# Gated linear attention beside a mixture of experts: the decays between tokens from broadcast loads and a bias, in place of a TensorE product

## The chip, the cores and the metric

One NeuronCore of a Trainium2 chip runs the whole kernel in one launch. The metric is device time in microseconds. The kernel before has a median of 1294.73 us over 9 runs (1287.51 to 1297.57). The engines are named as in the profile: PE is TensorE's matmul (PEld its weight load), DVE is VectorE, ACT is ScalarE, POOL is GpSimd, SP is SyncE, which here only issues DMAs.

## What is computed

The input x is (4, 2048, 256), so 8192 tokens of 256. It is layer-normed, and the output is x plus gated linear attention plus a mixture of experts, both of the normed x.

```python
# attention: 8 heads, keys of 128, values of 64, per sequence of 2048 tokens
q = (x @ Wq).reshape(B, S, H, DK)
k = (x @ Wk).reshape(B, S, H, DK) * DK ** (-0.5)
v = (x @ Wv).reshape(B, S, H, DV)
alpha = jax.nn.sigmoid((x @ Wg + bg) / GATE_NORM)      # one decay per token and head
def step(state, inp):
    qt, kt, vt, at = inp
    state = at[..., None, None] * state + kt[..., None] * vt[:, :, None, :]
    return state, jnp.einsum('bhk,bhkv->bhv', qt, state)
...
return out * sigmoid(x @ Wog) @ Wo
# experts: 64 experts, the 8 best of the 4 best groups per token, 256 places each
buf = zeros(E, CAP + 1, h).at[e, pos_c].set(x[token])[:, :CAP]
y = einsum('eci,eih->ech', silu(g) * u, w_down)
out = zeros(n, h).at[token].add(y_slots * w_slot[:, None])
```

With l(i) the sum of the log decays up to token i of a chunk of 128 tokens, the recurrence inside a chunk is a product of queries and keys, weighted by exp(l(i) - l(j)) for a query i and a key j that is not later than i, and by 0 for a later key. That weight, for four heads at a time, is the tile `dc` (128 keys on the partitions, 4 heads x 128 queries along them), and the change is about how `dc` is made.

## The kernel before, in words

The tokens go in 16 batches of 512 (`front`, `decays`, `back`: layer norm, routing, log decays) and, for the attention, in 32 blocks of 256 tokens, which are two chunks of 128 (`NCK`). A block has two halves of four heads. One *unit* is (block, half, chunk), 128 units in all. For each unit,

- `unit_l` (L889) makes `dc`,
- `unit_a` (L908) makes `sp`, keys times queries, in PSUM,
- `unit_m` (L921) multiplies `dc` by `sp` on VectorE (L924),
- `outputs` (L928) multiplies by the values (L940, result `od`) and adds the carried state times the decayed queries `qt` (L946); it takes two units at a time,
- `states` (L958) carries the state on.

**How `dc` is made before.** `decays` (L418) runs once for each of six groups of batches (1, 1, 2, 4, 4 and 4). The log decays z are split on a coarse grid into two parts (L433, L434). TensorE sums both parts over the tokens of a chunk (`cs`, L437 to L441); ScalarE takes the exponential of the running sum (`le`, for `el`) and of the sum from a token to the chunk's end (`w_end`). VectorE splits each running sum into three bf16 parts (`lt`, L453 to L457). TensorE transposes `le` and `lt`, VectorE copies them out of PSUM (`els` L462, `lts` L471), and SP stores them to DRAM (`el_d`, `lt_d`, L463 and L472). For each block, `load_block` (L778) brings the bf16 parts back with four small DMAs: into `aj` (key side, chunk by chunk) and into 6 rows of `mv` (query side; its other rows hold a fixed -1 per head). `unit_l` is then one bf16 matmul of 512 columns (L894) whose 54 rows add up l(i) - l(j) for four heads in PSUM (`lp`), a Relu with scale -1 (L898), which turns positive differences (later keys) into 0, and an Exp with scale -1 (L899). The mask for later keys is an `affine_select` on POOL (L904) as long as routing runs, and a multiplication by a triangle of ones on VectorE (L902) after that.

**Loads that stay.** `load_el` (L793) loads exp(l(i)) of four heads and two chunks as a broadcast to all 128 partitions: 512 KB a DMA, two DMAs a block. `queries` reads it (L855), and `wall` (L861) copies its last column for `states`, on POOL for the first 16 blocks and on VectorE from then on (`B["aux"]`).

**Order.** `block(s)` (L1026) writes out an order: attention of block s interleaved with projections of block s + 1, and between them `step()`, which advances the side work (layer norm, routing, decays) while there is any, and the experts after that. Block s + 1 is loaded at the head of block s (`load_block`, `load_el` of half 0) and in its middle (`load_el` of half 1). From this, the framework's scheduler makes one fixed list of instructions per engine, by priority and by a simulated time line, and each engine works its list strictly in order. So an instruction may stand well ahead of its place in the program, and one that has to wait holds up all that is behind it on its engine. SP's list holds nearly all loads and stores; POOL's queue issues the experts' gathers (L619) and their accumulating scatters (L697).

**Two long stages.** Up to some 605 us the attention runs beside layer norm and routing; then routing is done, and it runs beside the experts (`if "at" in moe`). PSUM's banks for the projections and `lp` (pool `pj`) are four in the first stage and three in the second. `dc` has a pool of its own with two buffers.

Of the kernel before, what the change touches and what calls it, by code (L numbers as in the profile page):

```python
# [19 lines left out]
P = 128  # L20
# [10 lines left out]
RT = 4  # L31
# [11 lines left out]
CGRID = 1.5 * 2.0 ** 14  # L43
# [5 lines left out]
NPART = 3  # L49
NJ = NPART * H  # L50
KL = 2 * NJ + 2 * NPART

# [19 lines left out]
def gla_moe_kernel(ctx: ExitStack, tc: tile.TileContext, x, Wq, Wk, Wv, Wo, Wg, bg, Wog,  # L72
# [17 lines left out]
    lt_d = [dram.tile([2 * NPART, H, RT, P], BF16, name=f"lt_d{b}") for b in range(NB)]  # L90
# [4 lines left out]
    identb = const.tile([P, P], BF16, name="identb")  # L95
    nc.vector.tensor_copy(identb, ident)
# [15 lines left out]
    w_end = const.tile([P, NB, H, RT], F32, name="w_end")  # L112
# [9 lines left out]


    mz = tmpc.tile([P, H], BF16, name="mz")
    nc.vector.memset(mz, 0.0)
    for q0 in (0, NJ + 2 * NPART):
        for m in range(NPART):
            nc.gpsimd.affine_select(out=mz, in_=mz, pattern=[[-1, H]],
                                    compare_op=ALU.not_equal, fill=-1.0, base=-(q0 + 8 * m),
                                    channel_multiplier=1)  # L130
    NM = 4

    mv_t = [const.tile([P, H, P], BF16, name=f"mv{i}") for i in range(NM)]
    aj_t = [const.tile([P, NCK, P], BF16, name=f"aj{i}") for i in range(2)]
    nc.gpsimd.tensor_copy(mv_t[0], bc(mz, 2, P))
    for t in aj_t:
        nc.vector.memset(t, 1.0)
# [111 lines left out]
    dcp = ctx.enter_context(tc.tile_pool(name="dcp", bufs=2))  # L249
# [33 lines left out]

    lad = r1.tile([P, RT, P], BF16, name="lad")
# [26 lines left out]
    zs = r1.tile([P, NB, H, RT], F32, name="zs")  # L311
    sg = r1.tile([P, NB, H, RT], F32, name="sg")
# [20 lines left out]
    def front(b):  # L333
# [75 lines left out]
        nc.vector.scalar_tensor_tensor(zs[:, b].rearrange("p h t -> p t h"), in0=lg[:, :, E:E + H],  # L409
# [8 lines left out]
    def decays(gi):  # L418

        b0, nb_ = DGROUPS[gi]  # L420
        n = nb_ * H * RT

        z = zs[:, b0:b0 + nb_].rearrange("p b h t -> p (b h t)")
        sm = sg[:, b0:b0 + nb_].rearrange("p b h t -> p (b h t)")
        nc.vector.tensor_scalar(sm, sm, SMIN, None, ALU.max)
        made["ln"] = nc.scalar.activation(sm, sm, AF.Ln).ins
        nc.vector.tensor_scalar(z, z, -UMIN, 0.0, ALU.add, ALU.min)
        nc.vector.tensor_scalar(z, z, LMIN - UMIN, None, ALU.max)
        yield True
        nc.vector.tensor_tensor(z, z, sm, ALU.add)  # L430

        g = dk.tile([P, 2, n], F32, tag="g", name="g")
        nc.vector.tensor_scalar(g[:, 0, :], z, CGRID, CGRID, ALU.add, ALU.subtract)  # L433
        made["g"] = nc.vector.tensor_tensor(g[:, 1, :], z, g[:, 0, :], ALU.subtract).ins  # L434
        yield True
        cs = ps["mo"].tile([P, 4, n], F32, tag="mo", name="cs")
        nc.tensor.matmul(cs[:, 0:2, :].rearrange("p a n -> p (a n)"), lhsT=u_le,  # L437
                         rhs=g.rearrange("p a n -> p (a n)"), start=True, stop=True)
        for q in range(2):
            nc.tensor.matmul(cs[:, 3, :], lhsT=u_le, rhs=g[:, q, :], start=(q == 0), stop=(q == 1))  # L440
        made["cs"] = nc.tensor.matmul(cs[:, 2, :], lhsT=u_gt, rhs=z, start=True, stop=True).ins  # L441

        le = dk.tile([P, n], F32, tag="le", name="le")
        made["le"] = nc.scalar.activation(le.rearrange("p (b t h) -> p b h t", b=nb_, t=RT),
                                          cs[:, 3, :].rearrange("p (b h t) -> p b h t", b=nb_, t=RT), AF.Exp).ins
        made["exp"] = nc.scalar.activation(w_end[:, b0:b0 + nb_].rearrange("p b h t -> p (b h t)"),
                                           cs[:, 2, :], AF.Exp).ins
        lt = dk.tile([P, 2, nb_, NPART, H * RT], BF16, tag="lt", name="lt")
        rs = dk.tile([P, 2, n], F32, tag="g", name="rs")
        by_batch = dict(b=nb_)  # L450
        c4 = cs[:, 0:2, :].rearrange("p a (b n) -> p a b n", **by_batch)
        r4 = rs.rearrange("p a (b n) -> p a b n", **by_batch)
        nc.vector.tensor_copy(lt[:, :, :, 0, :], c4)  # L453
        nc.vector.tensor_tensor(r4, c4, lt[:, :, :, 0, :], ALU.subtract)
        nc.vector.tensor_copy(lt[:, :, :, 1, :], r4)
        nc.vector.tensor_tensor(r4, r4, lt[:, :, :, 1, :], ALU.subtract)
        made["lt2"] = nc.vector.tensor_copy(lt[:, :, :, 2, :], r4).ins  # L457
        yield True
        ep = ps["mo"].tile([n, P], F32, tag="mo", name="ep")
        nc.tensor.transpose(ep, le, ident)  # L460
        els = dk.tile([n, P], F32, tag="ls", name="els")
        nc.vector.tensor_copy(els, ep)  # L462
        nc.sync.dma_start(out=el_d[gi], in_=els)  # L463
        NR = NPART * H * RT
        for i in range(nb_):
            b = b0 + i
            lp = ps["mo"].tile([NR, 2, P], BF16, tag="mo", name="ltp")
            for q in range(2):
                made["ltp"] = nc.tensor.transpose(lp[:, q, :], lt[:, q, i].rearrange("p a n -> p (a n)"), identb).ins
            lts = r2.tile([NR, 2, P], BF16, name="lts")  # L470
            made["lts"] = nc.vector.tensor_copy(lts, lp).ins  # L471
            made["lt"] = nc.sync.dma_start(out=lt_d[b].rearrange("(q a) h c i -> (a h c) q i", q=2), in_=lts).ins  # L472
            yield True
# [292 lines left out]
    def begin_block(s):  # L766
        blk[s] = dict(el=[None, None], wall=[None, None], q=[None, None], k=[None, None], kt=[None, None],
                      v=[None] * NCK, vw=[None] * NCK, oT=[None] * NCK)
        blk[s]["aux"] = nc.gpsimd if s < NB else nc.vector
        b, c0 = s // 2, (s % 2) * NCK  # L770
        if s == 0:
            xs = batch[0]["xT"][:, 0:NCK]
        else:
            xs = xsp.tile([P, NCK, 2, 2, P], F16, name="xs")
            nc.sync.dma_start(out=xs, in_=xT_d[b][:, c0:c0 + NCK])
        blk[s]["x"] = xs[:, :, 0], xs[:, :, 1]

    def load_block(s):  # L778
        if s:
            begin_block(s)  # L780
        b, c0 = s // 2, (s % 2) * NCK
        aj = aj_t[s % 2]
        lt = lt_d[b].rearrange("a h c i -> (a h) c i")
        nc.sync.dma_start(out=aj[0:NJ], in_=lt[0:NJ, c0:c0 + NCK, :])
        nc.sync.dma_start(out=aj[NJ + 2 * NPART:KL], in_=lt[NJ:2 * NJ, c0:c0 + NCK, :])
        mv = []
        for ck in range(NCK):
            t = mv_t[(s * NCK + ck) % NM]
            loaded = nc.sync.dma_start(out=t[NJ:NJ + 2 * NPART], in_=lt_d[b][:, :, c0 + ck, :])
            mv.append(t)  # L790
        blk[s].update(loaded=loaded, aj=aj, mv=mv)
# [32 lines left out]
    def values(s, ck):  # L824
# [11 lines left out]
        if (s * NCK + ck + 1) % (SEQ // P):  # L836
            vwh = vp_.tile([P, H, DV], F16, name="vwh")
            vwl = vp_.tile([P, H, DV], F16, name="vwl")
            vw = w1.tile([P, H, DV], F32, name="vw")
            B["aux"].tensor_tensor(vw, v, bc(w_end[:, b, :, c0 + ck], 2, DV), ALU.mult)  # L840
            nc.scalar.copy(vwh, vw)
            B["aux"].tensor_tensor(vwl, vw, vwh, ALU.subtract)
            B["vw"][ck] = (vwh, vwl)

# [44 lines left out]
    def unit_l(s, half, ck):  # L889

        B = blk[s]
        h0 = half * 4
        lp = ps["pj"].tile([P, 4, P], F32, tag="pj", name="lp")
        nc.tensor.matmul(lp.rearrange("p h i -> p (h i)"), lhsT=B["aj"][:, ck, :],  # L894
                         rhs=B["mv"][ck][:, h0:h0 + 4, :].rearrange("p h i -> p (h i)"),
                         start=True, stop=True)
        dc = dcp.tile([P, 4, P], F32, name="dc")
        nc.scalar.activation(dc, lp, AF.Relu, scale=-1.0)  # L898
        nc.scalar.activation(dc, dc, AF.Exp, scale=-1.0)  # L899

        if "at" in moe:
            nc.vector.tensor_tensor(dc, dc, bc(u_le, 1, 4), ALU.mult)  # L902
        else:
            nc.gpsimd.affine_select(out=dc, in_=dc, pattern=[[0, 4], [1, P]], compare_op=ALU.is_ge,  # L904
                                    fill=0.0, base=0, channel_multiplier=-1)
# [120 lines left out]
    def block(s):  # L1026
# [8 lines left out]
        if n:  # L1035
            load_block(s + 1)
            load_el(s + 1, 0)
        unit_l(s, 0, 1)
# [39 lines left out]
        load_el(s + 1, 1)  # L1078
        unit_l(s, 1, 1)
# [34 lines left out]
    for t in mv_t[1:]:  # L1114
        nc.sync.dma_start(out=t, in_=mv_t[0])
# [54 lines left out]
    with after(made["el"]):  # L1170
        load_block(0)
    with after(blk[0]["loaded"].ins):
        load_el(0, 1)
        nc.sync.dma_start(out=gbias, in_=gate_bias.partition_broadcast(P))
# [86 lines left out]
```

## Time and profile before

| | before |
|---|---|
| median of 9 runs | 1294.73 us |
| the profiled execution | 1291.28 us |
| its span, first to last instruction | 1289.6 us |
| mean granted TensorE clock | 0.996 |
| DMA traffic | 165.36 MB, mean 128 GB/s |
| share of 16 DMA engines: SP's queue, POOL's queue | 28.1%, 20.9% |
| small loads of the decay parts: aj<-lt_d, mv<-lt_d | 64 and 64, 12 KB each |
| broadcast loads: el<-el_d | 64, 512 KB each |

A profile is one execution. Its page gives the busy time of each engine, the chain of work that ended last, and the groups of instructions by source line. A group line reads: line, engine, operation, tile written and tiles read, shapes, count, then busy time, mean duration of one in ns, and the idle time of the engine just before them with what ended it. Matmuls are pipelined: what one costs is seen in the distance of starts, not in its duration. The other engines' back-to-back instructions overlap a little as well. Views of the trace beside the page are the timeline (instructions in order of time), the waits (who waited for whom), and windows (busy time of each engine in a stretch).

### The profile page before, as it was taken

The numbers are of one execution on the slowest core, as the hardware profiler recorded it, in microseconds if no ns is written. First come the engines' busy times: TensorE is split into PE (matmuls) and PEld (weight loads), VectorE is DVE, ScalarE is ACT, GpSimd is POOL, SyncE is SP. The second block draws the span as 40 slices with busy tenths as digits, with TensorE's granted clock in tenths as the row PEclk, the third lists the DMA queues.
The fourth block names the chain that finished last, engine by engine and source line by source line (L and its number), as shares of the span: only waits on it lengthen the run. The fifth ranks groups of instructions, "written<-read, shape, count | busy, mean of one in ns | idle before, by whom it ended". The sixth has DMA issues, their size and how long they took to land.

```text
span 1289.6 us, 34810 instructions
## 1 busy us (share of the span) xinstructions
PE 1205.1 (93%) x13782; PEld 1043.4 (81%) x13783; DVE 997.6 (77%) x2733; ACT 832.4 (65%) x1522; POOL 711.0 (55%) x885
## 2 busy tenths in 40 slices
PE   6789999988999999999899999999999999999997
PEld 6577877777877778788788888888888898888986
DVE  6976877776777777777878788788788897877864
ACT  4576666675666566655667666677677676666764
POOL 1476666664765666643427565636756556555330
PEclk9899999999999999999999999999999999999999
DMA  7534443343233443322646666567767677656531
GB/s 236 157 118 119 128 123 116 114 126 113 72 106 107 126 123 107 107 66 70 171 109 145 147 157 142 139 149 177 142 152 158 148 173 169 136 118 157 103 67 34
DMA packets 148580, 165.36 MB, mean 128 GB/s; under 512 B 32384, under 2 KB 119296, under 8 KB 147712
## 3 DMA queue, kind: packets, MB, share of 16 engines
q1 hardware_dynamic: 114896, 113.57, 28.1%
q0 software_dynamic: 29712, 45.89, 20.9%
q10 hardware_dynamic: 3808, 3.67, 0.8%
q8 instruction: 108, 1.77, 0.6%
q14 instruction: 56, 0.46, 0.1%
HBM read 115.98 MB, written 58.38 MB: 135 GB/s over the span
## 4 chain that ended last, share of the span: by engine, by line
PE 54%; DVE 17%; POOL 13%; ACT 6%; DMA 4%; issue 4%; SPq 1%; another core or an unknown queue 0%; ACTq 0%; POOLq 0%; DVEq 0%
PE pj L269 8%; PE pj L271 8%; PE pj L270 8%; PE od L940 3%; DMA el<-el_d 3%; PE od L946 3%; PE kp L879 2%; PE gu L271 2%; PE gu L269 2%; PE gu L270 2%; POOL ol L985 2%; POOL state L976 2%; PE xet L639 2%; DVE k L221 2%; DVE dc L924 2%
## 5 line engine op out<-in xcount | busy, mean ns | idle before, releaser
L697 POOL DMA_INDIRECT out_dram<-y,idx x128 | 209.8, 1639 | 98.1 <-DMA out_dram<-y,idx 27.5
L619 POOL DMA_INDIRECT xe<-xw_d,idx x128 | 138.2, 1080 | 149.7 <-ACT y L683 112.6
L269 PE MATMUL pj<-xs,wq_h 128*128 128x256 f16 x496 | 136.3, 275 | 5.6 <-ACT dc L898 4.2
L269 PE MATMUL pj<-xs,wk_h 128*128 128x256 f16 x496 | 135.2, 273 | 1.4 <-ACT dc L898 0.8
L270 PE MATMUL pj<-xs,wq_h 128*128 128x256 f16 x496 | 136.0, 274 | 0.0
L271 PE MATMUL pj<-xs,wq_l 128*128 128x256 f16 x496 | 135.9, 274 | 0.0
L270 PE MATMUL pj<-xs,wk_h 128*128 128x256 f16 x496 | 135.2, 273 | 0.8 <-issue 0.7
L271 PE MATMUL pj<-xs,wk_l 128*128 128x256 f16 x496 | 135.2, 273 | 0.1
L221 DVE SCALAR_TENSOR_TENSOR k<-pj,k 128x512 f16<-128x512 f32 x128 | 87.6, 684 | 46.9 <-ACT k L220 46.9
L924 DVE TENSOR_TENSOR dc<-sp,dc 128x512 f32<-128x512 f32 x128 | 87.7, 685 | 32.4 <-PE sp L271 14.6
L940 PE MATMUL od<-dc,v 128*64 128x128 f32 x1024 | 101.5, 280 | 10.4 <-DVE dc L924 9.6
L270 PE MATMUL sp<-ql,k 128*128 128x128 f16 x512 | 96.6, 220 | 15.5 <-DVE ql L221 15.3
L898 ACT ACTIVATE dc<-lp 128x512 f32<-128x512 f32 x128 | 76.1, 595 | 47.3 <-PE lp L894 21.6
L220 ACT ACTIVATE qh<-pj 128x512 f16<-128x512 f32 x128 | 74.7, 592 | 43.6 <-PE pj L271 33.4
L269 PE MATMUL sp<-qh,k 128*128 128x128 f16 x512 | 99.8, 220 | 3.1 <-issue 2.2
L220 ACT ACTIVATE k<-pj 128x512 f16<-128x512 f32 x128 | 75.2, 590 | 42.1 <-PE pj L271 37.4
L271 PE MATMUL sp<-qh,k 128*128 128x128 f16 x512 | 96.5, 220 | 0.7 <-issue 0.7
L946 PE MATMUL od<-qt,state 128*64 128x128 f32 x960 | 93.9, 273 | 0.0
L879 PE MATMUL kp<-identh,k 128*128 128x128 f16 x1024 | 84.5, 221 | 9.3 <-DVE k L221 6.6
L221 DVE SCALAR_TENSOR_TENSOR ql<-pj,qh 128x512 f16<-128x512 f32 x128 | 86.6, 677 | 3.4 <-ACT qh L220 3.3
L855 DVE SCALAR_TENSOR_TENSOR qt<-pj,el 128x512 f32<-128x512 f32 x128 | 86.6, 677 | 0.0
L834 ACT ACTIVATE v<-pj 128x512 f32<-128x512 f32 x64 | 38.2, 598 | 74.4 <-PE pj L271 66.6
(409 smaller groups left out, 4524.0 us busy)
## 6 DMA issues: line engine op xcount, KB each, us to landing
el<-el_d SPq DMA_DIRECT2D x64, 512.0 KB
xw_d<-x SPq DMA_DIRECT2D x16, 512.0 KB
xT_d<-xT SPq DMA_DIRECT2D x16, 512.0 KB
out_dram<-in_L_attn_x_dram SPq DMA_DIRECT2D x16, 512.0 KB
w<-in_L_ffn_w_gate_dram SPq DMA_DIRECT2D x64, 128.0 KB
w<-in_L_ffn_w_up_dram SPq DMA_DIRECT2D x64, 128.0 KB
w<-in_L_ffn_w_down_dram SPq DMA_DIRECT2D x64, 128.0 KB
xs<-xT_d SPq DMA_DIRECT2D x31, 256.0 KB
```

The lines of the kernel that those rows point to most:

```text
L220: return (nc.scalar.activation(hi, t, AF.Copy, scale=scale).ins, nc.vector.scalar_tensor_tensor(lo, in0=t, scalar=scale, in1=hi, op0=ALU.m ...
L221: nc.vector.scalar_tensor_tensor(lo, in0=t, scalar=scale, in1=hi, op0=ALU.mult, op1=ALU.subtract).ins)
L269: nc.tensor.matmul(out_, lhsT=a[0], rhs=b[0], start=first, stop=False)
L270: nc.tensor.matmul(out_, lhsT=a[0], rhs=b[1], start=False, stop=False)
L271: return nc.tensor.matmul(out_, lhsT=a[1], rhs=b[0], start=False, stop=last).ins
L619: in_turn(lambda: nc.gpsimd.indirect_dma_start(out=xe[:, f, :], out_offset=None, in_=xw_d[:, :], in_offset=bass.IndirectOffsetOnAxis(ap=id ...
L697: two = [in_turn(lambda: nc.gpsimd.indirect_dma_start(out=of, out_offset=bass.IndirectOffsetOnAxis(ap=idx[:, e, f:f + 1], axis=0), in_=m[" ...
L855: read = nc.vector.scalar_tensor_tensor(qt, in0=pj, scalar=QFIT, in1=two_heads(el, i), op0=ALU.mult, op1=ALU.mult)
L879: nc.tensor.transpose(kp[:, i, :], k[:, i, :], identh)
L924: anchor.append(nc.vector.tensor_tensor(dc, B["sp"], dc, ALU.mult).ins)
L940: mm = nc.tensor.matmul(od[i * DV:(i + 1) * DV, n, j, :], lhsT=v[:, h0 + 2 * j + i, :], rhs=dc[:, 2 * j + i, :], start=True, stop=first)
L946: mm = nc.tensor.matmul(od[i * DV:(i + 1) * DV, n, j, :], lhsT=state[half][:, 2 * j + i, :], rhs=qt[:, ck, 2 * j + i, :], start=False, sto ...
```

## The change

The log decays are no longer split. `decays` computes, from z itself, the running sums `cs[1]` (for `el`), the sums to the chunk's end `cs[0]` (for `w_end`), and a third sum with the matrix `uq`: the key's own term, relative to the start of the quarter of the chunk (32 tokens) in which the key lies. The third is kept in SBUF for all tokens (`nl`). One more fp32 product per group, with the matrix `tq` of 4 x 128 columns, gives for each quarter g the log decay sums from the start of quarter g to every query i. These go to DRAM (`la_d`) and are loaded for each block and half as `la`: the partitions of quarter g get the rows of quarter g, broadcast to 32 partitions, four DMAs and 512 KB in all. `dc` is then a part of `la` itself: the mask is set first (POOL's `affine_select` fills with -30000, VectorE takes the minimum with a matrix of +30000 and -30000), and ScalarE's Exp adds `nl` as a per-partition bias, one instruction for each head, as the bias differs by head. The clamp of positive differences is gone. The arrays z, sg and `w_end` change the order of their last two dimensions. `load_block`, `aj`, `mv` and their set-up and the pool of `dc` go; `la` has a pool of three buffers.

```diff
-    dcp = ctx.enter_context(tc.tile_pool(name="dcp", bufs=2))
+    lap = ctx.enter_context(tc.tile_pool(name="lap", bufs=3))
...
+    later_ = const.tile([P, P], F32, name="later")
+    nc.vector.tensor_scalar(later_, u_le, -2.0 * NONE, NONE, ALU.mult, ALU.add)
...
+    tq = r1.tile([P, GQ, P], F32, name="tq")
+    for g in range(GQ):
+        nc.vector.tensor_scalar(tq[:, g], u_le, u_le[:, g * Q:g * Q + 1], None, ALU.subtract)
+    uq = r1.tile([P, P], F32, name="uq")
+    nc.vector.tensor_tensor(uq.rearrange("p (g i) -> p g i", g=GQ), bc(u_le[:, 0:P:Q], 2, Q),
+                            u_le.rearrange("p (g i) -> p g i", g=GQ), ALU.subtract)
...
         nc.vector.tensor_tensor(z, z, sm, ALU.add)
-        g = dk.tile([P, 2, n], F32, tag="g", name="g")
-        nc.vector.tensor_scalar(g[:, 0, :], z, CGRID, CGRID, ALU.add, ALU.subtract)
-        made["g"] = nc.vector.tensor_tensor(g[:, 1, :], z, g[:, 0, :], ALU.subtract).ins
         yield True
-        cs = ps["mo"].tile([P, 4, n], F32, tag="mo", name="cs")
...
+        cs = ps["mo"].tile([P, 3, n], F32, tag="mo", name="cs")
+        for k, u in enumerate((u_gt, u_le, uq)):
+            made["cs"] = nc.tensor.matmul(cs[:, k, :], lhsT=u, rhs=z, start=True, stop=True).ins
...
-        nc.vector.tensor_copy(lt[:, :, :, 0, :], c4)
-        nc.vector.tensor_tensor(r4, c4, lt[:, :, :, 0, :], ALU.subtract)
-        nc.vector.tensor_copy(lt[:, :, :, 1, :], r4)
-        nc.vector.tensor_tensor(r4, r4, lt[:, :, :, 1, :], ALU.subtract)
-        made["lt2"] = nc.vector.tensor_copy(lt[:, :, :, 2, :], r4).ins
+        made["lt2"] = nc.vector.tensor_copy(nl[:, b0:b0 + nb_].rearrange("p b t h -> p (b t h)"), cs[:, 2]).ins
...
-        for i in range(nb_):
...
-            for q in range(2):
-                made["ltp"] = nc.tensor.transpose(lp[:, q, :], lt[:, q, i].rearrange("p a n -> p (a n)"), identb).ins
-            lts = r2.tile([NR, 2, P], BF16, name="lts")
-            made["lts"] = nc.vector.tensor_copy(lts, lp).ins
-            made["lt"] = nc.sync.dma_start(out=lt_d[b].rearrange("(q a) h c i -> (a h c) q i", q=2), in_=lts).ins
-            yield True
+        lp = ps["mo"].tile([n, GQ, P], F32, tag="mo", name="lap")
+        made["ltp"] = nc.tensor.matmul(lp.rearrange("n g i -> n (g i)"), lhsT=z,
+                                       rhs=tq.rearrange("p g i -> p (g i)"), start=True, stop=True).ins
+        las = dk.tile([n, GQ, P], F32, tag="las", name="las")
+        made["lts"] = nc.vector.tensor_copy(las, lp).ins
+        made["lt"] = nc.sync.dma_start(out=la_d[gi].rearrange("g n i -> n g i"), in_=las).ins
+        yield True
...
-    def load_block(s):
...
+    def load_la(s, half):
         b, c0 = s // 2, (s % 2) * NCK
...
+        la = lap.tile([P, NCK, 4, P], F32, name="la")
+        gi = max(i for i, g in enumerate(DGROUPS) if g[0] <= b)
+        r0 = ((b - DGROUPS[gi][0]) * RT + c0) * H
+        src = la_d[gi][:, r0:r0 + NCK * H, :].rearrange("g (c h) i -> g c (h i)", h=H)[:, :, half * 4 * P:(half + 1) * 4 * P]
+        for g in range(GQ):
+            blk[s]["loaded"] = nc.sync.dma_start(out=la[g * Q:(g + 1) * Q].rearrange("p c h t -> p c (h t)"),
+                                                 in_=src[g].partition_broadcast(Q))
+        blk[s]["la"][half] = la
...
     def unit_l(s, half, ck):
         B = blk[s]
-        h0 = half * 4
-        lp = ps["pj"].tile([P, 4, P], F32, tag="pj", name="lp")
-        nc.tensor.matmul(lp.rearrange("p h i -> p (h i)"), lhsT=B["aj"][:, ck, :],
-                         rhs=B["mv"][ck][:, h0:h0 + 4, :].rearrange("p h i -> p (h i)"),
-                         start=True, stop=True)
-        dc = dcp.tile([P, 4, P], F32, name="dc")
-        nc.scalar.activation(dc, lp, AF.Relu, scale=-1.0)
-        nc.scalar.activation(dc, dc, AF.Exp, scale=-1.0)
+        b, c = s // 2, (s % 2) * NCK + ck
+        dc = B["la"][half][:, ck]
         if "at" in moe:
-            nc.vector.tensor_tensor(dc, dc, bc(u_le, 1, 4), ALU.mult)
+            nc.vector.tensor_tensor(dc, dc, bc(later_, 1, 4), ALU.min)
         else:
             nc.gpsimd.affine_select(out=dc, in_=dc, pattern=[[0, 4], [1, P]], compare_op=ALU.is_ge,
-                                    fill=0.0, base=0, channel_multiplier=-1)
+                                    fill=NONE, base=0, channel_multiplier=-1)
+        for i in range(4):
+            hh = half * 4 + i
+            nc.scalar.activation(dc[:, i], dc[:, i], AF.Exp, bias=nl[:, b, c, hh:hh + 1])
         B["dc", half, ck] = dc
...
     def block(s):
...
         if n:
-            load_block(s + 1)
+            begin_block(s + 1)
             load_el(s + 1, 0)
+            load_la(s + 1, 0)
...
         load_el(s + 1, 1)
+        load_la(s + 1, 1)
...
-    for t in mv_t[1:]:
-        nc.sync.dma_start(out=t, in_=mv_t[0])
...
     with after(made["el"]):
-        load_block(0)
+        load_la(0, 0)
     with after(blk[0]["loaded"].ins):
         load_el(0, 1)
+        load_la(0, 1)
```

## The prediction

> **What bounds the kernel now.** I read the busy times first, then the chain of work that ended last, then the same chain by stage, and only then the groups of instructions that the change touches. In the first fence the columns after each engine are its busy time and its instructions.
>
> ```profile
> PE 1205.1 (93%) x13782; PEld 1043.4 (81%) x13783; DVE 997.6 (77%) x2733; ACT 832.4 (65%) x1522; POOL 711.0 (55%) x885
> ...
> PE 54%; DVE 17%; POOL 13%; ACT 6%; DMA 4%; issue 4%; SPq 1%; another core or an unknown queue 0%; ACTq 0%; POOLq 0%; DVEq 0%
> ...
> 60.00:605.00 545.00, 507.94 (x6109) 428.92 (x6107) 408.41 (x1238) 347.81 (x613) 337.65 (x582) 1.00 0.38 109
> 605.00:1290.00 685.00, 655.21 (x7310) 578.43 (x7309) 542.70 (x1343) 453.10 (x856) 355.65 (x263) 1.00 0.60 138
> ```
>
> The last two lines are the windows view of the two long stages (length, then busy time of PE, PEld, DVE, ACT and POOL, the granted clock, the DMA share, GB/s): attention with routing, then attention with the experts. PE looks 93 to 96% busy in both, but they have different limits. When I add up the pieces of the chain by stage, PE makes 565.5 of the 685 us (83%) of the late stage, DVE 52.6 (8%) and ACT 24.2. In the middle stage PE makes only 112.7 of 545 (21%), POOL 163.6 (30%), DVE 156.1 (29%), ACT 43.8 (8%) and DMA 31.4, of which 28.1 is the load of el. So TensorE work is worth its time late, and a fifth of it in the middle.
>
> The decay step of a unit (one chunk, four heads) is these lines:
>
> ```profile
> L894 PE MATMUL lp<-mv,aj 128*128 128x512 bf16 x127 | 48.7, 383 | 0.0
> L898 ACT ACTIVATE dc<-lp 128x512 f32<-128x512 f32 x128 | 76.1, 595 | 47.3 <-PE lp L894 21.6 <-PE yp L271 9.4 <-PE pj L271 5.5
> L899 ACT ACTIVATE dc<-dc 128x512 f32<-128x512 f32 x128 | 80.8, 631 | 2.3
> L902 DVE TENSOR_TENSOR dc<-dc,u_le 128x512 f32<-128x512 f32 x63 | 43.2, 685 | 4.2 <-ACT dc L899 3.6 <-issue 0.3
> L904 POOL TENSOR_SCALAR_AFFINE_SELECT dc<-dc 128x512 f32<-128x512 f32 x65 | 42.5, 660 | 35.4 <-ACT dc L899 35.4
> L924 DVE TENSOR_TENSOR dc<-sp,dc 128x512 f32<-128x512 f32 x128 | 87.7, 685 | 32.4 <-PE sp L271 14.6 <-POOL dc L904 14.2 <-PE gu L271 2.4
> ```
>
> The relay PE, ACT, ACT, POOL or DVE, DVE, PE is visible in the idle columns: each engine waits for the one before it.
>
> **What TensorE gives up.** 383 ns is not the price of the product, as matmuls overlap. The timeline has starts:
>
> ```profile
> 901.64 0.38 PE L894 MATMUL lp<-mv,aj 128*128 128x512 bf16 x1
> 901.86 0.27 PE L269 MATMUL pj<-xs,wk_h 128*128 128x256 f16 x1
> ```
>
> The next one starts 0.22 us later; the median over all is 0.216. 128 x 0.217 = 27.8 us, some 13.5 in the middle (62 units) and 13.7 late (63). By the chain's shares that is 13.7 x 0.83 = -11.3 and 13.5 x 0.21 = -2.8. Ends: 0 and -27.8.
>
> **Waits that go.** With no lp, no PSUM bank is held until ScalarE reads it, and the exponential no longer stands behind TensorE. Matmuls that waited for it: od on the product of L924 (PE idle 9.6 us), pj on L898 (5.0). Ends 0 and -14.6; I take a quarter, -4, since such idle time mostly comes back at the next wait.
>
> **The preparation (decays).** Removed on VectorE are the grid split and the three-part split and 16 copies: L433, L434, L453 to L457, L471, in all 19.4 us. Added are 6 copies of 512 columns out of PSUM (nearest: 0.67 us for 64x512 in L542) and 6 small ones (0.22, as L453): 5.3. Net 14 us in the middle, x 0.29 = -4 (ends 0, -14). On TensorE 32 transposes (4.1 us) go and 6 products of 512 fp32 columns come (two 256-column fp32 rows of 282 ns each, 3.4 us): nothing, and they would be 3 us if uncovered.
>
> **ScalarE.** Before: Relu and Exp of 512 columns, which start 0.478 and 0.536 us apart in a row: 1.01 us. After: four Exp of 128 columns with a per-partition bias. No row has that shape. From below: L683 (256 columns, one per-partition operand, from PSUM) steps 0.356 us; from above: L382 (256 columns, two such operands, from SBUF) steps 0.492. 128 columns less are 0.11 us (512 columns more cost 0.44 between L886 and L884), so 0.25 to 0.38 each, 1.0 to 1.53 for four. I take 0.30, between them, as there is one operand but an SBUF source: 1.2, so +0.19 x 128 = +24 us of work (ends 0, +66). ScalarE is 65% busy and has 8% and 3.5% of the chain, so +1.3; all +24 if its idle time were gone.
>
> The Trainium skill (ScalarE: Activation LUTs, "What ACT_TABLE_LOAD costs") speaks against this change: a per-partition operand adds about 93 ns to each instruction, and a small one is mostly fixed cost. By its figures four take 1.18 us and the old pair 1.04, which would be +18 us of work, an estimate; the rows above bracket it, so the sum would stay.
>
> **The loads.** Removed are two 12 KB loads into aj and two into mv per block; added are 64 times 512 KB into la, in four DMAs of 32 partitions. The nearest row is el: also 512 KB, 256 packets of 2,048 bytes, and packets of that size took 102 ns on average in the trace, so 256 x 102 / 16 = 1.64 us of all 16 DMA engines, 105 us over the run. The DMA share rises from 0.38 to about 0.46 and from 0.60 to 0.68: room in both. el's last packet ends 3.2 to 4.5 us behind its issue. On SP, eight issues of 0.37 a block (3.0 us) replace 2.2. They wait for the buffer's last reader, od, and behind them queue the experts' weights; those that were issued at 909 to 911 were used by ScalarE at 918.5, so 7 us cover that. I take +1; ends 0 and +12.6, the chain's whole DMA time late, again.
>
> **The wait that comes.** The mask now comes first, on POOL in the middle and on VectorE late, and depends on nothing but la's landing. What such an instruction does is seen at el: the copy wall on POOL is ordered as early as its load was thought to be there, and POOL stands still.
>
> ```profile
> 100.35 0.36 SPq L799 DMA_DIRECT2D el<-el_d  x1
> ...
> 105.31 0.19 POOL L861 COPY wall<-el 128x8 f32<-128x8 f32 x1 [1.23 <-DMA el<-el_d]
> 105.47 1.16 POOL L842 TENSOR_TENSOR vwl<-vw,vwh 128x512 f16<-128x512 f32 x1
> ...
> POOL wall L861: 33.1, 21
> ```
>
> 33.1 us over 32 loads of el in that stage is 1.03 us a load. Queued behind it are vwl, state and ol, which feed TensorE. If la's first reader waits as long: 32 x 1.03 = 33 us on POOL, x 0.30 = +10; late, 33 us on VectorE, x 0.08 = +2.5. Ends: 0 (la has three buffers and is needed half a block later, so the mask may well be placed late) and +66 (each wait whole on the path). VectorE's instruction itself, min for mult, keeps its 685 ns; POOL's select its 660.
>
> **Start-up.** The first product of L924 starts at 49.5, after POOL's wait for el until 48.6. The split chain goes, 1 MB more of broadcasts comes early. I take -2; ends -5 (the first lp ran at 43.9, and POOL was free to follow at once) and +6.6 (four more loads of 1.64).
>
> **Sum**: -11.3 - 2.8 - 4 - 4 + 1.3 + 1 + 10 + 2.5 - 2 = -9.3. The profiled execution took 1291.3 us (span 1289.6 and 1.7 around it), so 1282.0. It lies 3.4 below the median of the nine runs, 1294.7; for a median I add them: **1285**.
>
> **Rivals.** *All of TensorE's time comes out*: la always lands before anyone looks. For it: the late stage is 83% PE, el there has no wait on VectorE. Against it: VectorE is 79% busy late. 1294.7 - 27.8 - 4 - 2 = 1261. *No change*: VectorE and POOL set the pace as soon as TensorE lets go. For it: 21% in the middle. Then -11.3 is halved and the waits take the rest: 1292 to 1297. *Slower by in-order waits*: la's first reader stops POOL and VectorE at each load, as wall does, and lands later than el, behind it in the queue. The gains are 24.1, the other costs 2.3, so it decides from 21.8 / 64 = 0.34 us a load on the path. With half of the 66 us on the path, 1294.7 - 21.8 + 33 = 1306; with all, 1339. For it: el alone makes 28 us of the middle chain. Against it: POOL's 35.4 us of waiting for L899 go at the same places. *The exponentials do not get cheaper for anyone*: at 1.53 us a unit with its share doubled, +7, 1292; inside "no change".
>
> **Chances.** Forecast 0.40 (1274 to 1290), all of it 0.12, no change 0.10, slower 0.38. Faster by more than 0.3% (about what a measurement of this kernel can tell from no change; 3.9 us) 0.52, within 0.10, slower 0.38. The range goes from just under the full gain, 1258, into the slower case to where some three quarters of la's waits are on the path, 1322.
>
> **What would show it.** Right: no lp; PE busy near 1156 (1205 - 49); a group of 512 exponentials with a mean near 0.4 us; POOL's wait for L899 gone; the late stage shorter by 8 us or more. The wait: idle time before the select (POOL) and the min (VectorE) that a DMA of la ended, 33 us each by my figure. Wrong: if that idle time is over 60 us, or if the weights' wh waits for w by more than its 3.5 us, SP's queue being the cause.

## The result, and the profile after

| | before | after |
|---|---|---|
| median | 1294.17 us (62 runs) | 1364.07 us (19 runs) |
| lowest to highest | 1287.33 to 1302.33 | 1352.78 to 1373.18 |
| span of the profiled execution | 1289.6 us | 1368.0 us |
| mean granted TensorE clock | 0.996 | 0.976 |

The change makes the kernel slower by 5.2%: the ratio is 1.0523, 95% interval [1.0506, 1.0539]. One of the 19 runs after, the highest, was in a slower state, and the ratio is that of the means of the fast runs (that of the two medians is 1.054). The forecast was 1285 with a range up to 1322, so the sign was wrong and the time lies outside the range.

The page of the kernel after, busy times:

```profile
PE 1216.7 (89%) x13623; PEld 1043.3 (76%) x13623; DVE 1003.8 (73%) x2689; ACT 838.4 (61%) x1778; POOL 708.9 (52%) x878
```

TensorE has 159 matmuls less, and yet its busy time is 11.6 us longer; I had expected 49 us less. No engine has become the bound: every busy share fell. What grew is idle time, and with it the time in which TensorE runs at a lower clock.

The windows view of the two long stages, with the columns as in the prediction:

```profile
60.00:605.00 545.00, 489.09 (x5851) 411.89 (x5849) 403.61 (x1160) 338.31 (x712) 329.00 (x573) 0.98 0.48 137
605.00:1290.00 685.00, 618.04 (x6679) 537.76 (x6677) 514.85 (x1307) 427.05 (x918) 345.01 (x261) 0.98 0.65 155
```

In the same 685 us TensorE gets 6679 matmuls done where it did 7310 before. The DMA shares, 0.48 and 0.65, are about what I had forecast (0.46 and 0.68). Starts of the product `dc` times `sp` (L924 before, L891 after) show where time is lost: the first of the 128 starts 2.7 us earlier than before (46.7 against 49.5), the 65th 18.8 later (628.0 against 609.1), the last 74.9 later (1355.3 against 1280.4). So the loss grows over the whole run, and three quarters of it lies in the late stage.

The groups of the decay step, each with the idle time of its engine just before it and what ended it:

```profile
L872 ACT ACTIVATE la<-la,nl 128x128 f32<-128x128 f32 x512 | 160.3, 390 | 108.7 <-POOL la L868 52.4 <-DVE la L866 48.3 <-issue 5.7
L891 DVE TENSOR_TENSOR la<-sp,la 128x512 f32<-128x512 f32 x128 | 87.5, 684 | 37.7 <-PE sp L257 31.3 <-PE kp L849 3.2 <-ACT la L872 2.6
L866 DVE TENSOR_TENSOR la<-la,later 128x512 f32<-128x512 f32 x63 | 41.1, 688 | 51.1 <-DMA la<-la_d 48.6 <-issue 2.4
L868 POOL TENSOR_SCALAR_AFFINE_SELECT la<-la 128x512 f32<-128x512 f32 x65 | 40.8, 649 | 25.2 <-DMA la<-la_d 24.4 <-PE pj L257 0.4 <-issue 0.3
L849 PE MATMUL kp<-identh,k 128*128 128x128 f16 x1024 | 89.5, 222 | 46.0 <-DVE k L207 43.3 <-ACT k L206 0.8 <-ACT res L964 0.5
```

The instructions cost what they should: min 688 ns, select 649, an exponential 390. The waits are the news. VectorE stands still for 48.6 us until a load of la lands, POOL for 24.4; ScalarE, whose exponential is next in its own list, stands still behind them for 52.4 + 48.3 = 100.7 us; and TensorE waits 43.3 us for `k`, which VectorE copies out of PSUM once it is free again. In the kernel before, ScalarE's step waited for TensorE (36.5 us in the three reasons shown), VectorE's mask 3.6 us for ScalarE, and TensorE's `kp` 6.6 us for `k`:

```profile
L879 PE MATMUL kp<-identh,k 128*128 128x128 f16 x1024 | 84.5, 221 | 9.3 <-DVE k L221 6.6 <-ACT dc L898 2.0 <-ACT res L997 0.4
```

The worst of these stops (the second in this fence), in the chain of work that ended last (start, length, what). SP issues the four DMAs of one la, and from then on the chain runs through their landing:

```profile
1064.31 0.45 SPq L759
1064.80 4.50 DMA la<-la_d
1069.42 0.70 DVE la L866
...
1088.33 0.38 SPq L759
1088.75 0.64 SPq L759
1089.43 1.70 SPq L759
1091.18 10.55 DMA la<-la_d
...
1102.46 0.95 DVE wl L683
1103.41 0.60 DVE la L866
```

Above it stands the load before, where the landing takes 4.50 us of the chain; here it takes 10.55. The same moment in the timeline, first VectorE, then TensorE:

```profile
1093.76 0.15 DVE L580 TENSOR_TENSOR idx<-row,place 128x2 int32<-128x2 f32 x1
1101.85 0.69 DVE L866 TENSOR_TENSOR la<-la,later 128x512 f32<-128x512 f32 x1 [7.94 <-DMA la<-la_d]
...
1097.35 0.27 PE L257 MATMUL pj<-xs,wq_l 128*128 128x256 f16 x1
1106.53 1.01 PE L849 MATMUL kp<-identh,k 128*128 128x128 f16 x8 [8.91 <-DVE k L207]
...
1108.19 0.41 PE L256 MATMUL gu<-xel,wh 128*128 128x256 f32 x1
1108.40 0.41 PE L257 MATMUL gu<-xeh,wl 128*128 128x256 f32 x1
```

VectorE idles 7.94 us for a mask whose weights are multiplied only at 1138.9, 37 us later. Behind the mask stands the copy that makes `k`; TensorE's next instruction reads it, and TensorE idles 8.91 us. When it goes on, the matmuls of `gu` start 0.21 us apart; at 1059.8 they started 0.12 apart. The clock records show half clock from 1100.8 on for 10.2 us.

### The profile page after: what moved, and what is told of

It reads as the page before. It is cut to its first block, busy times and chain, and to the rows that moved or that the text cites. A ratio compares the mean times of both kernels' runs of the same rounds, so it can differ in the third digit from the quotient of the medians.

```text
span 1368.0 us, 35132 instructions
## 1 busy us (share of the span) xinstructions
PE 1216.7 (89%) x13623; PEld 1043.3 (76%) x13623; DVE 1003.8 (73%) x2689; ACT 838.4 (61%) x1778; POOL 708.9 (52%) x878
## 3 DMA queue, kind: packets, MB, share of 16 engines
q1 hardware_dynamic: 128000, 145.04, 35.4%
## 5 line engine op out<-in xcount | busy, mean ns | idle before, releaser
L872 ACT ACTIVATE la<-la,nl 128x128 f32<-128x128 f32 x512 | 160.3, 390 | 108.7 <-POOL la L868 52.4
L849 PE MATMUL kp<-identh,k 128*128 128x128 f16 x1024 | 89.5, 222 | 46.0 <-DVE k L207 43.3
L891 DVE TENSOR_TENSOR la<-sp,la 128x512 f32<-128x512 f32 x128 | 87.5, 684 | 37.7 <-PE sp L257 31.3
L255 PE MATMUL sp<-qh,k 128*128 128x128 f16 x512 | 99.7, 222 | 15.5 <-ACT qh L206 11.2
L849 PEld LDWEIGHTS <-k 128*128 128x128 f16 x1024 | 67.2, 99 | 59.2 <-DVE k L207 36.9
L907 PE MATMUL od<-la,v 128*64 128x128 f32 x1024 | 102.6, 280 | 10.7 <-DVE la L891 9.9
L951 ACT CAST oh<-oT 128x512 fp32r<-128x512 f32 x64 | 39.5, 617 | 115.6 <-DVE oT L921 105.8
L921 DVE SCALAR_TENSOR_TENSOR oT<-og,od 128x256 f32<-128x256 f32 x128 | 48.6, 415 | 57.2 <-PE od L913 29.1
```

Of the source, the lines that this page charges most:

```text
L255: nc.tensor.matmul(out_, lhsT=a[0], rhs=b[0], start=first, stop=False)
L849: nc.tensor.transpose(kp[:, i, :], k[:, i, :], identh)
L872: nc.scalar.activation(dc[:, i], dc[:, i], AF.Exp, bias=nl[:, b, c, hh:hh + 1])
L891: anchor.append(nc.vector.tensor_tensor(dc, B["sp"], dc, ALU.mult).ins)
L907: mm = nc.tensor.matmul(od[i * DV:(i + 1) * DV, n, j, :], lhsT=v[:, h0 + 2 * j + i, :], rhs=dc[:, 2 * j + i, :], start=True, stop=first)
```

## The experiments

**The theories.** Theory 1: order. The masks are the first readers of la, and they stand in VectorE's and POOL's lists where the planned time line has la landed: in the run that is 4 to 10 us after la's first issue for 63 of the 64 loads, and mostly 20 to 55 us before the product that needs the result. As each list is worked strictly in order, VectorE, POOL and, behind them, ScalarE stop at every load. Rivals: the loads cost the time by contention and by the queue; ScalarE's four exponentials cost it; TensorE's relief is worth nothing.

Kernels that are compared ran on one chip with the kernel before, and ratios are to its runs there; its median was 1266.71 us on one chip and 1294.71 and 1292.6 in the other two sets. A point below is 1% of the kernel before's time; where ratios of different sets are subtracted, it is taken for granted that a ratio is the same on every chip. The expectations in us were written for the kernel before's 1294 us; on that scale hold_both comes to 1272, hold_late to 1306, before_loads to 1304 and exp_one to 1352.

**Both masks held back (hold_both).** An ordering alone: each mask is put behind the product of `dc` and `sp` that was traced last before it (L891 of the changed kernel), on VectorE in the order of issue, on POOL by a wait for that product.

```diff
-            nc.vector.tensor_tensor(dc, dc, bc(later_, 1, 4), ALU.min)
+            with tc.issue_after(anchor[-1]):
+                nc.vector.tensor_tensor(dc, dc, bc(later_, 1, 4), ALU.min)
...
-            nc.gpsimd.affine_select(out=dc, in_=dc, pattern=[[0, 4], [1, P]], compare_op=ALU.is_ge,
-                                    fill=NONE, base=0, channel_multiplier=-1)
+            masked = nc.gpsimd.affine_select(out=dc, in_=dc, pattern=[[0, 4], [1, P]], compare_op=ALU.is_ge,
+                                             fill=NONE, base=0, channel_multiplier=-1).ins
+            if anchor:
+                tc.add_manual_dep(masked, anchor[-1].name, mybir.DependencyInfo(
+                    mybir.DependencyClass.Sync, mybir.DependencyReason.DATA), reason="hold")
```

> The changed kernel, with one thing added: the mask of a unit is ordered behind the product (sp times dc) that was traced last before it, one or two units ahead of its own, on VectorE by issue order and on POOL by a dependency. Theory 1 (early reader: the mask stands in its engine's list at the landing of la that the scheduler simulated, the chip's landing is later, so VectorE or POOL and then ScalarE stand still, and TensorE's clock falls after it): nearly all of the loss comes back, 1265 to 1300 us, idle time before the masks under 10 us (73 before), half-clock time of TensorE near that of the kernel before. Theory 2 (32 MB more on the DMA engines slow everything) and theory 3 (512 small exponentials cost ScalarE too much): the order doesn't matter to them, 1345 us or more.

Measured: 1245.26 us against 1266.71, ratio 0.9832 [0.9816, 0.9849]. The same instructions and the same loads, in another order, are by these ratios 6.6% faster than the changed kernel and 1.7% faster than the one before. The page and the late stage of this kernel:

```profile
PE 1178.8 (95%) x13623; PEld 1026.1 (83%) x13623; DVE 990.0 (80%) x2689; ACT 841.8 (68%) x1779; POOL 715.2 (58%) x878
...
605.00:1230.00 625.00, 619.97 (x7025) 552.79 (x7024) 515.25 (x1275) 441.89 (x956) 357.21 (x257) 1.00 0.71 166
```

TensorE is busy 99% of the late stage at full clock. In its waits the loads of la hardly appear:

```profile
ACT la L876 <- POOL la L869: 3.5, 3, 2.5
...
DVE la L867 <- DMA la<-la_d: 3.3, 1, 3.3
...
ACT la L876 <- DVE la L867: 2.1, 3, 1.4
...
POOL la L869 <- DMA la<-la_d: 1.6, 1, 1.6
```

And the timeline of VectorE shows two masks right behind a product and with no idle time. The second of them is the first read of a load that was issued from 967.5 on, 17.5 us earlier.

```profile
983.75 0.69 DVE L895 TENSOR_TENSOR la<-sp,la 128x512 f32<-128x512 f32 x1 [0.62 <-PE sp L257]
984.36 1.28 DVE L867 TENSOR_TENSOR la<-la,later 128x512 f32<-128x512 f32 x2
985.56 0.69 DVE L812 TENSOR_TENSOR vwl<-vw,vwh 128x512 f16<-128x512 f32 x1
```

**One engine's masks at a time (hold_late: VectorE's; hold_early: POOL's).** Each is one half of the edit above.

> The same hold for the mask on VectorE alone, the late stage; POOL's masks stay where they are. Product number 64 came 19 us later than in the kernel before, and the other 56 us were lost behind it. Theory 1: the late part of the loss comes back, 1300 to 1325 us, product 64 still near 628. If the late loss has another cause: 1345 or more.

> The changed kernel with the hold on POOL's masks alone (the first stage); VectorE's masks stay at the landing. If the two stages lose for themselves, this gives back what the hold on VectorE left: ratio to the kernel before about 1.024 to 1.032 (hold on VectorE alone 1.009, changed kernel 1.052, both 0.983). If the early stalls only push the late ones along, 1.045 or more.

Measured: hold_late 1277.39 against 1266.71, ratio 1.0088 [1.0071, 1.0105]; hold_early 1326.19 against 1294.71, ratio 1.0280 [1.0222, 1.0338]. In each, one of the two waits is left, as the waits of hold_late and of hold_early show:

```profile
ACT la L873 <- POOL la L869: 44.3, 23, 4.9
...
POOL la L869 <- DMA la<-la_d: 19.8, 13, 4.1
...
DVE la L867 <- DMA la<-la_d: 3.2, 1, 3.2
```

```profile
DVE la L866 <- DMA la<-la_d: 47.6, 22, 7.7
ACT la L875 <- DVE la L866: 47.6, 25, 8.4
...
POOL la L868 <- DMA la<-la_d: 1.6, 1, 1.6
```

From 1.0523, holding POOL's masks gives 2.4 points and holding VectorE's 4.35; together 6.8, and both at once give 6.9. So the two waits add up within the interval of hold_early (0.6 points each way), and neither was covered by other work.

The edges change the engines' lists elsewhere as well. But the loss stays in the stage whose masks still wait, as the starts of the 128 products of `dc` and `sp` show; the masks of the first 65 are POOL's, those of the other 63 VectorE's (us, profiled execution):

| kernel | first to 65th | 65th to last |
|---|---|---|
| before | 559.7 | 671.3 |
| after | 581.2 | 727.3 |
| hold_both, one chip | 542.5 | 642.5 |
| hold_late, the same chip | 576.5 | 642.5 |
| hold_wall (both masks held, see below), another chip | 547.0 | 668.0 |
| hold_early, the chip of hold_wall | 541.1 | 720.4 |

With POOL's masks left at the landing (hold_late), 34.0 us are lost up to the 65th product and none behind it; with VectorE's left there (hold_early), 52.4 us are lost behind it and none before.

**The loads alone (before_loads).** The kernel before, with as many bytes of broadcast loads for each block and half as la has, 512 KB, here in eight DMAs of 64 KB (four of 32 partitions for each unit, from `el_d`) in place of la's four of 128 KB; nobody reads them.

```diff
+        la = lap.tile([P, 4, P], F32, name="la")
+        with tc.issue_after(made["el"]):
+            for g in range(4):
+                nc.sync.dma_start(out=la[g * 32:(g + 1) * 32].rearrange("p h t -> p (h t)"),
+                                  in_=el_d[0][4 * g:4 * g + 4, :].rearrange("h i -> (h i)").partition_broadcast(32))
```

> The kernel before, computing as it did, with 128 times 256 KB more of broadcast loads (four DMAs of 32 partitions each) into a tile that nothing reads: the traffic of la without its readers. Theory 1: the loads alone cost little, 1290 to 1310. Theory 2: the traffic and SP's queue are the loss, 1340 or more.

Measured: 1275.62 against 1266.71, ratio 1.0074 [1.0057, 1.0091]. The traffic costs 0.7%, about 9 us. It is a real term, and far from 5.2%.

**One exponential for four (exp_one).** The changed kernel with one Exp of 512 columns; the key's own sum is left out of the exponent.

```diff
-        for i in range(4):
-            hh = half * 4 + i
-            nc.scalar.activation(dc[:, i], dc[:, i], AF.Exp, bias=nl[:, b, c, hh:hh + 1])
+        nc.scalar.activation(dc, dc, AF.Exp)
```

> The changed kernel with one Exp of 512 columns in place of four of 128 with a bias; it leaves out the key's own sum in the exponent. ScalarE's work falls by some 80 us. Theory 3: 1290 to 1320. Theory 1: ScalarE still waits for the mask and the mask for la, 1345 to 1365.

Measured: 1322.58 against 1266.71, ratio 1.0444 [1.0414, 1.0474]. ScalarE is busy 72 us less (766.7), and 0.8 points come back. The stops stay, as the groups show:

```profile
L870 ACT ACTIVATE la<-la 128x512 f32<-128x512 f32 x128 | 78.1, 629 | 113.8 <-DVE la L866 73.4 <-POOL la L868 40.1
L866 DVE TENSOR_TENSOR la<-la,later 128x512 f32<-128x512 f32 x63 | 41.4, 690 | 75.2 <-DMA la<-la_d 75.2
```

**la by one DMA (one_dma).** The changed kernel, la loaded by one DMA of 128 partitions from the rows of quarter 0; the rows of the other three quarters are left out.

```diff
-        for g in range(GQ):
-            blk[s]["loaded"] = nc.sync.dma_start(out=la[g * Q:(g + 1) * Q].rearrange("p c h t -> p c (h t)"),
-                                                 in_=src[g].partition_broadcast(Q))
+        blk[s]["loaded"] = nc.sync.dma_start(out=la.rearrange("p c h t -> p c (h t)"),
+                                             in_=src[0].partition_broadcast(P))
```

> The changed kernel with la loaded by one DMA of 128 partitions with the rows of quarter 0 in place of four DMAs of 32 partitions; the other quarters' rows are left out, so the sums of three quarters of the keys are not the right ones. Bytes and order rules stay. Theory 1 (the masks stand where the planned time line thinks la has landed, and wait for the real landing): the four issues of 0.37 us are part of what the landing takes on the chip; with one issue the plan moves the mask forward as well, so some of the wait stays: between 30 and 65 us of VectorE and POOL idle before the masks by la's DMA, ratio 1.025 to 1.048. Rival (the loss has nothing to do with how and when la lands, but with the masks' and exponentials' own work): 1.050 to 1.054, idle as before. If the four-DMA shape were the whole cause: 0.98 to 0.99.

Measured: 1341.13 against 1292.6, ratio 1.0402 [1.0363, 1.0441]. Its waits:

```profile
DVE la L865 <- DMA la<-la_d: 41.2, 21, 5.0
...
POOL la L867 <- DMA la<-la_d: 11.2, 13, 2.1
```

Splitting the load in four is a part of it (1.2 points), and the stops remain without the split.

**TensorE's work put back (hold_pe).** hold_both, with an fp16 product of 512 columns for each unit in the pool `pj`, which nobody reads, in place of the bf16 product that the change took away.

```diff
+        lp = ps["pj"].tile([P, 4, P], F32, tag="pj", name="lp")
+        nc.tensor.matmul(lp.rearrange("p h i -> p (h i)"), lhsT=B["x"][0][:, ck, 0, :],
+                         rhs=wparts["wv"][0][:, 0, :], start=True, stop=True)
```

> Both masks held, and one fp16 product of 512 columns per unit put back on TensorE beside it, into the PSUM pool that lp had, read by nobody: the TensorE work that the change removes. If TensorE's time is worth what the forecast said (14 us of 27.8), the ratio goes from 0.983 to 0.994 (0.990 to 0.998); if all of it counts, 1.005; if the gain of the held version comes from the shorter relay instead, it stays at 0.983 to 0.987.

Measured: 1292.7 against 1294.71, ratio 0.9988 [0.9962, 1.0015], that is 1.56 points above hold_both, or 20 us. This lies just above what was expected. But it is not a clean price of TensorE's time: on the chip of hold_wall the first stage takes 574.4 us to the 65th product, 27 more than there, for some 14 us of products, and the second takes 657.9, 10 less. In the first stage waits are back: ScalarE stands 19.8 us behind POOL's masks (3.5 in hold_both), and POOL's `wall` 23.2 us for el (10.7). So the 20 us are the product together with what it does to the order and to the banks of `pj`; no run separates them.

**One exponential where nothing stops (hold_exp_one).** hold_both and the edit of exp_one together; the key's own sum is left out.

> Both masks held behind the last traced product, and one Exp of 512 columns without a bias in place of four of 128 with one; the key's own sum is left out of the exponent. It prices the four exponentials where no early wait hides it. Theory 1 (ScalarE has room, 61% busy): ratio 0.978 to 0.984, that is at most 0.5% under the 0.983 of the four exponentials. Rival (ScalarE stands on the path once the waits are gone): 0.965 to 0.977, the 65 to 70 us of ScalarE's work that go being worth 10 us or more.

Measured: 1247.75 against 1292.6, ratio 0.9654 [0.9623, 0.9685]. Theory 1 missed here: ScalarE's 75 us of work (766.9 busy against 841.8) are worth 1.8 points, 23 us, or 0.31 us for each us. That ScalarE is busy 68% of the span does not make its work free.

**The other early reader (before_wall, hold_wall).** The copy `wall` on POOL reads el as early as the masks read la. Here it waits, in the first stage, until VectorE has read el; once in the kernel before, once in hold_both.

```diff
-                B["aux"].tensor_copy(wall, el[:, :, :, P - 1])
+                copied = B["aux"].tensor_copy(wall, el[:, :, :, P - 1]).ins
+            if s < NB:
+                tc.add_manual_dep(copied, read.ins.name, mybir.DependencyInfo(
+                    mybir.DependencyClass.Sync, mybir.DependencyReason.DATA), reason="hold")
```

> The kernel before with its own reader of a load held: POOL's copy wall waits for VectorE's read of the same el in the first stage. If such early readers cost what the chain shows for el (28 us in the middle stage), 0.980 to 0.988; if POOL had time to spare, 0.995 to 1.003.

> Both masks held and the copy wall as well. Idle time before wall was 10.7 us with the masks held. If that still counts, 0.975 to 0.981; if not, 0.982 to 0.985 like without it.

Measured: before_wall 1281.94 against 1294.71, ratio 0.9905 [0.9874, 0.9936]; hold_wall 1272.09 against 1294.71, ratio 0.9835 [0.9802, 0.9869]. The kernel before had the same weakness and pays about 12 us for it, somewhat less than theory 1 said. POOL's idle time before `wall` is not less for it: it waits 40.0 us for VectorE's read in before_wall, where it waited 33.1 us for el. So an idle time is not a price by itself; what is queued behind it, and when that is due, decides. In hold_both there is nothing left to win, perhaps because there POOL's wait for el had already fallen to 10.7 us (35.1 after); why was not tried. Against before_wall, which has el's reader in order too and ran on the same chip, hold_wall is 0.993: with the order settled in both, the change itself brings some 0.7%.

The waits before the masks, side by side (idle time ended by a load of la, us):

| kernel | VectorE | POOL | ratio |
|---|---|---|---|
| after | 48.6 | 24.4 | 1.0523 |
| exp_one | 75.2 | 27.3 | 1.0444 |
| one_dma | 41.2 | 11.2 | 1.0402 |
| hold_early | 47.6 | 1.6 | 1.0280 |
| hold_late | 3.2 | 19.8 | 1.0088 |
| hold_both | 3.3 | 1.6 | 0.9832 |

hold_both beats both kernels, and of the kernels that leave nothing out it is, with hold_wall, the fastest that ran.

## Why the prediction was wrong

**The wait that comes (+10 and +2.5; ends 0 and +66): the step that failed.** What would happen was named: la's landing stops POOL and VectorE at their masks, as el's stops `wall`. The amount of idle time was close as well: 73.0 us, where I had 33 for each. What failed is the weight. I multiplied the idle time by each engine's share of the chain before (0.30 and 0.08), so that 66 us became 12.5. On the chip the order is worth 6.9 points, 89 us of 1294: as much as all of the idle time or more, not a fifth of it. VectorE's 45.4 us (48.6 less 3.2) are worth 4.35 points, 56 us. POOL's 22.8 (24.4 less 1.6) are worth 2.4 points, 31 us, but there `wall`'s wait for el went as well (35.1 us after, 8.6 in hold_early), so the price of one us of POOL's stop cannot be told from it. Up to 12 of the 89 us may belong to `wall`.

A chain share tells how often an engine's work set the end in the old balance. A new stop does not meet that balance: with VectorE stopped, ScalarE's next instruction waits for VectorE, and TensorE waits for `k`, whose copy stands behind the mask. The groups show this at one place after the other (48.6 on VectorE, 48.3 on ScalarE behind it, 43.3 on TensorE behind `k`). I had named what stands behind POOL's `wall`, but not that ScalarE's exponential would stand behind each mask, in order ahead of the copies out of PSUM. Nor had I counted a second price, the clock; it follows below. That VectorE's stops cost more than their idle time I put down to both; no run separates them.

**The bound of +66** was wrong with it: "each wait whole on the path" was no upper end, and the range ended at 1322 for that reason, with three quarters of that.

**The sign of the rival.** "Slower by in-order waits" is what came true, with its place. It decides from 0.34 us a load on the path; 73.0 us over 64 loads are 1.14. Its highest price, 1339, was still 25 us short. My argument against it, that POOL's 35.4 us of waiting for L899 go at the same places, did come true in part: no such wait is left. But a wait for ScalarE's exponential comes when the result is nearly due, and the wait for la comes 20 to 50 us before that.

**"la ... may well be placed late"** (the lower end) was wrong: with three buffers and half a block of lead, the mask still stands at the load's expected landing. The lead that the buffers give was never used, since the first reader moves forward with the load.

**TensorE (-11.3 and -2.8).** The sign agrees with hold_pe, and the size was small beside its 20 us. But the product that was put back costs its time in the first stage, where I had -2.8, and none in the second, where I had -11.3, and waits come back with it. What TensorE's time alone is worth stays open.

**ScalarE (+1.3).** The new duration was right: four exponentials in a row take 1.28 us in the trace, 0.29 from start to start, where I took 0.30. The old one was misread: 0.478 is the distance from the Relu to the next instruction when that is another one; in 77 of the 128 units the Exp follows directly and starts 0.62 us later. So the change added less than the 24 us of work: ScalarE's busy time grew by 6.0 us (9.4 in hold_both). The weight was too low: at 0.31 us for each us of work (hold_exp_one) that makes 2 to 3. This is worked out, not run.

**Loads and SP (+1, ends 0 and +12.6).** 0.74% of 1294, 9.6 us (before_loads): inside the ends, near the upper one. The weights' `wh` waits for `w` 6.0 us, more than the 3.5 that I had named as a limit, but 2.5 us are a small part of this loss.

**Start-up (-2).** The first product starts 2.7 us earlier in the profiled execution.

**Waits that go and the decays (-4 and -4)** were not run by themselves. The measured terms are -20 + 9.6 + 3 + 89 = 81.6, and the change made the kernel 69.9 us slower by the medians, so some -12 is left for these, for start-up and for `wall`, as far as terms from different kernels may be added and the -20 is TensorE's.

**Of what was to show it**: no lp, exponentials near 0.4 us and the wait for L899 gone came true. PE busy near 1156 did not (1216.7), nor the shorter late stage. "If that idle time is over 60 us" was the mark of a wrong forecast, and it is 73.

## What to carry to other kernels

When an instruction that computes on a loaded tile no longer depends on a late engine, ask where the scheduler will put it: likely at the expected landing of the load, far ahead of its use, and there its engine and everyone behind it wait for the real one. Tie such a first reader to the step before its use (here an ordering edge, 1.0523 to 0.9832, with no other change). And do not weigh a new stop on an engine that empties PSUM by that engine's share of the old chain of waits: here each us of VectorE's stop cost 1.2 us, where its share had said 0.08.

## What the runs showed of the hardware

TensorE's clock is a second price of short stops. In the clock records from 60 us on, the kernel before has one piece at half clock, of 3.4 us; the one after has 14, of 54.6 us in all, hold_early 41.0, hold_late 27.3 and hold_both 10.2 (a piece that runs past the last instruction is left out). In such a piece work takes up to twice as long (`gu` above: 0.21 us from start to start against 0.12), so at most half of the 51 us more is lost time, some 26 us of the 70. It is not the whole price: exp_one has 71.6 us at half clock and is the faster of it and the kernel after. Each piece of the kernel after was one or more times 3.4 us long, and 13 of the 14 came after 2.0 to 4.6 us without a matmul in the 10 us before.

The Trainium skill (TensorE: Matmul & The Clock Gate, "Part 1: The HAM clock gate") says that the array falls to half its clock after an idle window of about 3.4 us and comes back after a busy one. The length of the pieces agrees. The idle time needed does not always: in the kernel after, in the 10 us before the clock fell at 339.7 the longest gap between matmuls was 1.40 us (2.0 us of gaps in all), before 377.2 it was 2.08 (3.0 in all), and before 1025.8 0.38 (1.1 in all), as far as the modelled ends of matmuls show gaps.

A load's landing is not steady either: in the kernel after, the four DMAs of one la were issued from 1088.3 to 1091.2 and released VectorE at 1101.9, 10.7 us after the last, while for those of 1063.5 to 1064.8 the last took 4.5 us. Both come to 512 KB on the same queue. The DMA records show what stood beside the slow one: from 1089 to 1095 POOL's queue, with the add `out_dram<-at_d` (L978, issued at 1086.7), moved 0.99 MB and took 85.4% of the time of the 16 DMA engines, SP's queue took 5.9%, and la's packets of 2,048 bytes begin only at the end of that.
